# Decoder of two layers on one core: the first attention's value products one step later behind their moves, a layer norm one group later, and the rest of an entmax eight products into the experts' first step

## The chip, the cores and the metric

The kernel runs on one core of one Trainium2 chip. A core has five engines with a queue of instructions each: TensorE (PE, matrix products; its loads of stationary operands are listed as PEld), VectorE (DVE), ScalarE (ACT), GpSimd (POOL) and SyncE (SP, which here only issues transfers). Transfers (DMAs) are issued from SP or ACT and moved by 16 DMA engines. The metric is the device time of one execution in microseconds (us), lower is better; the figure of a kernel is the median of its runs. One further execution is recorded by the hardware profiler, and that is the profile and trace read here.

## The reference, cut to what matters

Two sequences of 1024 tokens of width 256 pass through six blocks, each followed by a residual and a layer norm, all in float32: attention, cross attention with an MLP, a mixture of experts, then attention, cross attention and a quantised MLP. The change touches the first three.

```
x = layernorm(x + attn(x))        # attn(x) itself returns x + z
    q, k, v = 16 heads of 64;  weights = softmax(q k^T / 8);  z = (weights v) w_o
x = layernorm(x + xattn(x, ctx))  # one head, 64 context tokens
    out = softmax(q k^T) v;  gelu(out W1 + b1) W2 + b2
x = layernorm(x + experts(x))     # 8 experts, hidden width 1024
    gates = entmax(x Wr + br)     # alpha = 1.5, by bisection
    y_e = relu(x W1_e + b1_e) W2_e + b2_e;  out = sum_e gates_e y_e
```

## The kernel before, in words

**First attention (`l0_attn`, L206).** The 16 heads of a sequence are taken two at a time; such a pair of heads of one sequence is a unit `u`, 16 in all. A unit has eight steps of 128 queries; there are 128 steps `n`. A step's work for its 128 queries and both heads is:

- `scores`: eight matrix products into two wide PSUM tiles (L297);
- `most`: two row maxima on DVE (L312); `exponentials`: two exponentials on ACT, with row sums (L317); `divided`: a reciprocal on DVE (L325) and two divisions on POOL (L328);
- `turn`: two transposes of 32 by 32 blocks on DVE into `blocks` (L342), of which there are two buffers, each for two steps.

Two steps make one pair `m`. After the second step's `turn`, `move` brings the 32 by 32 blocks into place for a product, `turned`, of which there are two buffers too: of sixteen copies over partitions twelve are DMAs of 128 KB (ten issued from SP, L358, two from ACT, L360), two are copies on POOL (L362), and two are kept for `stays`, which does one on ACT (L367) and one on POOL (L368) a step later. `mix(m)` is the value product: 32 products of PE into one PSUM bank `acc` (L379), evacuated by ACT into `aoT` (helper L74).

`others` holds work that is due at a numbered step (the `at(...)` calls): the projections of q and k of the next unit, one 512-token block at a time (`project`, L252), each followed by two DMAs from SP that shift one head's rows to the other half of the partitions (L266, for k only after its second block); its values (L276); weight loads from SP (L237); output products (L396) whose sums DVE takes (L402, L404); the layer norm's `finish`, and `onward`, the transposes of a normed group for the next stage (helpers: moments L178 to L183, the power L183 on POOL, scaling L200, transposes on PE L157).

The main loop (L490 to L509) writes this order out by hand for PE, DVE, ACT and POOL. At step `n` it emits `scores`, `most` and `exponentials` of `n + 2`, `turn` of `n + 1`, `divided` of `n + 2`; and then by parity:

```
if n % 2:
    stays()
    mix((n - 3) // 2)
else:
    others(n - 1)
    others(n)
    move(n + 1)
```

So pair `m` is moved at step 2m and multiplied at step 2m + 3. Below, a step is called even or odd by this `n`. SP's queue takes its DMAs in the order of this text. The last `mix` and four outputs are kept in `self.left_over`, and the last two groups' `finish` and `onward` in `self.ends`.

**Cross attention (`l0_xattn`, L577).** Four groups `g` of 512 tokens. PE's order is by hand: first layer `up` (L648) in four pieces, second layer `down` (L661, sums on DVE L665) in four pieces, with the next group's softmax, transposes and value products between them. The entmax of the first sequence's router (`entmax`, L740 on) is a generator that yields between stretches of DVE work; `self.rest` is that generator. In group 2 the kernel takes four stretches of it by `some()`; the third ends with a power on POOL (L791), and the next on DVE begins with L793, which reads it.

**Experts (`l0_ffn`).** 32 steps (8 experts by 4 groups), each with 21 places in a hand-written order of products; at a place, a job from a table can be put behind the product. At step 0 the table holds the rest of the first entmax, the last group's transposes and router product (`last_group`), and four pieces of `begin(0)`, which turns the gates on PE (L873) and starts the accumulators. `tokens` prepares the groups' Strassen sums.

Of the kernel before, what the change touches and what calls it, by code (L numbers as in the profile page):

```python
# [33 lines left out]
class Decoder:  # L34
# [181 lines left out]
    def l0_attn(self):  # L216
# [5 lines left out]
        with ExitStack() as s:  # L222
# [123 lines left out]
            def move(n):  # L346
                m, qt = divmod(n, 2)
                if qt == 0 or not 0 <= n < steps:
                    return
                to = turned[m] = tp.tile([P, 8, 4, P], F32, tag="turned", name="turned")  # L350
                src = blocks.pop(m).rearrange("p (k r) h t q -> p k r (h t q)", r=4)
                moves = [
                    (to[32 * r : 32 * r + 32, :, i, :], src[32 * i : 32 * i + 32, :, r, :])
                    for d in range(4) for i in range(4) for r in [(i + d) % 4]
                ]
                few = 6 if n == steps - 1 else 2
                for b, a in moves[4 : 16 - few]:
                    nc.sync.dma_start(b, a)  # L358
                for b, a in moves[16 - few :]:
                    nc.scalar.dma_start(b, a)  # L360
                for b, a in moves[:2]:
                    nc.gpsimd.tensor_copy(b, a)  # L362
                stay.extend(moves[2:4])
# [6 lines left out]
            def mix(m):  # L370

                if m < 0:
                    return
                u, qb = divmod(m, 4)
                av = self.acc()
                for kt in range(8):
                    p = turned[m][:, kt].rearrange("p i (h t q) -> p h i t q", h=2, t=2)
                    for h in range(2):
                        nc.tensor.matmul(  # L379
                            av[own[h], 0:256].rearrange("p (t i q) -> p i t q", t=2, i=4),  # L380
                            lhsT=vals[u][:, kt, own[h]], rhs=p[:, h], start=kt == 0, stop=kt == 7,
                        )
                if qb == 0:
                    aT[u] = aop.tile([P, S], F32, tag="aoT", name="aoT")
                self.evac(aT[u][:, qb * 256 : (qb + 1) * 256], av[:, 0:256], by=nc.scalar)
# [36 lines left out]
            steps = B * NP * 8  # L422
# [38 lines left out]
            def others(n):  # L461
                for f, args in extra.pop(n, ()):
                    f(*args)
# [5 lines left out]
            with self.tc.manual_schedule(engines=engines):  # L469
                def begin(n):  # L470
                    scores(n)
                    for f in (most, exponentials):
                        for h in range(2):
                            f(n, h)
                    divided(n)

                for n in (-12, -11):
                    others(n)
                for k, i in ((1, 0), (1, 1), (0, 0)):
                    project(0, k, i)  # L480
                begin(0)
                project(0, 0, 1)
                for n in (-10, -8, -6, -4, -2):
                    others(n)
                for i in range(2):
                    values(0, i)
                begin(1)
                for i in range(2, 4):
                    values(0, i)
                for h in range(2):  # L490
                    turn(0, h)
                nc.sync.dma_start(wo, t["L0_attn_w_o"].rearrange("(g p) d -> p g d", p=P))
                next(constants)
                for n in range(steps):
                    scores(n + 2)
                    for h in range(2):
                        most(n + 2, h)
                        exponentials(n + 2, h)
                    for h in range(2):
                        turn(n + 1, h)  # L500
                    divided(n + 2)
                    if n % 2:
                        stays()
                        mix((n - 3) // 2)
                    else:
                        others(n - 1)
                        others(n)
                        move(n + 1)
            assert not extra  # L509

            self.left_over = [lambda: mix(steps // 2 - 1)] + [
# [65 lines left out]
    def l0_xattn(self):  # L577
# [5 lines left out]
        with ExitStack() as s:  # L583
# [113 lines left out]
            with self.tc.manual_schedule(engines={mybir.EngineType.PE}):  # L697
                with self.tc.high_priority(400):
                    softmax(0)
                    for job in self.left_over:  # L700
                        job()
                    turn(0)
                    mix(0)
                queries(0)
                for g in range(NG):
                    up(g, 0)
                    up(g, 2)
                    some()
                    onward(g - 1)
                    queries(g + 1)  # L710
                    some()
                    if g == 0:
                        for job in self.ends:
                            job()
                    up(g, 4)
                    softmax(g + 1)
                    some()
                    up(g, 6)
                    logits(g - 1)
                    if g > 0:  # L720
                        self.xT[g - 1] = xT[g - 1]
                    if g in (1, 2):
                        self.tokens(g - 1)
                    if g == 2:
                        self.rest = self.entmax(0)
                        steps = islice(self.rest, 4)
                    some()
                    down(g, 0)
                    turn(g + 1)
                    some()  # L730
                    down(g, 1)
                    mix(g + 1)
                    some()
                    down(g, 2)
                    some()
                    down(g, 3)
# [101 lines left out]
    def l0_ffn(self):  # L838
        nc, t = self.nc, self.t
        HT = GT // 2  # L840
        with ExitStack() as s:
# [157 lines left out]
            with self.tc.manual_schedule(engines=engines):  # L999
                start = [begin(b) for b in range(B)]  # L1000
                mixed = None
                for n in range(len(steps) + 1):
                    jobs = {}
                    for k in range(4):
                        if n == 3:
                            jobs[k] = lambda: next(start[1])
                    if n == 0:
                        jobs[0] = lambda: [None for _ in self.rest]
                        jobs[3], jobs[6] = self.last_group
                        for k in range(7, 11):  # L1010
                            jobs[k] = lambda: next(start[0])
                    for k in {1: (4, 7, 10, 13), 2: (8, 12)}.get(n, ()):
                        jobs[k] = lambda: next(gates)
                    if n > 3:
                        jobs[14] = lambda: next(ready, None)
                    if n >= len(steps) - NG + 2:
                        g = n - (len(steps) - NG + 2)
                        if n < len(steps):
                            jobs[5], jobs[17] = (lambda: normed(g)), (lambda: turned(g))
                    a = hidden(*steps[n]) if n < len(steps) else None  # L1020
                    b = gather(*steps[n - 1], mixed) if n else None
                    if n % NG == 1 and n // NG + 1 < E:
                        load(n // NG + 1)
                    for i, k in enumerate(order):
                        if isinstance(k, int):
                            if b:
                                b(k)
                        elif a:
                            a(*k)
                        if i in jobs:  # L1030
                            jobs[i]()
                    if n == 0:
                        for _ in start[0]:
                            pass
                        self.tokens(2)
                        self.tokens(3)
                    if n == 2:
                        for _ in gates:
                            pass
                    if n % NG == NG - 1 and n // NG + 1 < E:  # L1040
                        first(n // NG + 1)
                    if n % NG == 0 and 0 < n < len(steps):
                        second(n // NG)
                    if a:
                        mixed = sums(*steps[n])
                for _ in ready:
                    pass
                for g in range(2, NG):
                    normed(g)
# [743 lines left out]
```

## Time and profile before

| | us |
|---|---|
| median of 3 runs | 2489.21 (2487.06 to 2491.77) |
| profiled execution | 2493.86 |
| its span in the trace | 2492.0 |
| mean granted clock of PE | 0.968 |
| PE busy, of the span | 2346.6 |
| DVE, ACT, POOL busy | 1686.2, 1107.1, 909.8 |

The span runs from the first to the last instruction in the trace; the 1.9 us beside it are start and end of the execution. The stages and PE's busy time in them:

| stretch of the span (us) | what runs there | PE busy (us) | share of the DMA engines |
|---|---|---|---|
| 0 to 40 | loads, first projections | 30.08 | 0.63 |
| 40 to 787 | first attention | 705.27 of 747 | 0.81 |
| 787 to 957 | first cross attention | 158.13 of 170 | 0.09 |
| 957 to 1560 | experts | 600.58 of 603 | 0.07 |
| 1560 to 2492 | second layer | 852.56 of 932 | 0.13 |

How the page and the trace's answers are read: in a group's row stand line, engine, operation, written tile, read tile, shapes and count, then busy time and the mean of one in ns, then the engine's idle time ahead of these instructions and what ended most of it. A row of waits has engine, tile and line, then what it waited for, then us in total, times and the longest; "SPq" is SP's queue. A row of the timeline begins with start and duration in us and ends with the idle time before it and what ended it, in brackets. A row of transfers ends with the size and the median us from issue to landing.

### The profile page before, as it was taken

To read this page: it belongs to the slowest core of one execution; us is meant where nothing else is said; L and a number is where in the kernel's file an instruction comes from. 1 tells how busy PE (TensorE), PEld (TensorE's weight loads), DVE (VectorE), ACT (ScalarE), POOL (GpSimd) and SP (SyncE) were. 2 spreads that over 40 slices of the span, in tenths; PEclk is the share of its full clock that TensorE was granted. 3 is DMA by queue.
4 is the path that set the end of the run, shared out by engine and by line. 5 is a ranking of instruction groups with operands and counts; after the bars stand their busy time and mean duration, and the time that the engine had idled before them with its cause. 6 is when DMAs were issued, how large, how long until landed. Compare 5 with 4: busy or idle time off the path is not lost. (4 is left out here: it accounts for less than half of the span.)

```text
span 2492.0 us, 37380 instructions
## 1 busy us (share of the span) xinstructions
PE 2346.6 (94%) x14062; PEld 1603.8 (64%) x14065; DVE 1686.2 (68%) x2934; ACT 1107.1 (44%) x1730; POOL 909.8 (37%) x747
## 2 busy tenths in 40 slices
PE   8999999999998989999999999999889999998974
PEld 4455545455555658899999999999734444444742
DVE  5888788887784334555555555546678787985786
ACT  4565565565552212233333333333136555663344
POOL 4666666566566122342343342423201001002412
PEclk9999999999999999999999999999979999999995
DMA  7888788787887001010010010100212222300001
GB/s 166 163 160 165 152 174 169 139 164 153 161 161 165 1 0 41 1 39 26 13 35 30 18 46 1 47 5 1 42 26 35 35 35 35 53 16 1 1 1 34
DMA packets 275668, 168.79 MB, mean 68 GB/s; under 512 B 47560, under 2 KB 262176, under 8 KB 275488
## 3 DMA queue, kind: packets, MB, share of 16 engines
q1 hardware_dynamic: 239072, 148.05, 28.6%
q10 hardware_dynamic: 36416, 18.36, 3.7%
q8 instruction: 111, 1.82, 0.3%
q14 instruction: 69, 0.57, 0.1%
HBM read 34.21 MB, written 2.10 MB: 15 GB/s over the span
## 5 line engine op out<-in xcount | busy, mean ns | idle before, releaser
L312 DVE TENSOR_REDUCE nm<-wide 128x1 f32<-128x1024 f32 x256 | 301.3, 1218 | 121.9 <-PE wide L297 120.2
L1160 DVE TENSOR_REDUCE most<-bank 128x1 f32<-128x512 f32 x512 | 325.6, 683 | 56.4 <-PE bank L1154 48.0
L1203 ACT ACTIVATE w<-wide 128x1024 f32<-128x1024 f32 x256 | 248.3, 1022 | 139.1 <-PE wide L1197 130.5
L379 PE MATMUL acc<-turned,v 128*64 128x256 f32 x2048 | 241.3, 389 | 30.0 <-DMA turned<-blocks 14.7
L297 PE MATMUL wide<-k,q 64*128 64x512 f32 x1024 | 258.4, 619 | 9.0 <-ACT p L317 8.3
L317 ACT ACTIVATE p<-wide,nm 128x1024 f32<-128x1024 f32 x128 | 142.6, 1114 | 238.1 <-DVE nm L312 150.0
L328 POOL TENSOR_SCALAR p<-p,sums 128x1024 f32<-128x1024 f32 x128 | 143.2, 1118 | 276.7 <-DVE sums L325 276.7
L379 PEld LDWEIGHTS acc<-turned,v 128*64 128x64 f32 x2048 | 155.5, 140 | 136.4 <-issue 42.7
L906 ACT ACTIVATE mhT<-mhT,cols 128x256 f32<-128x256 f32 (+1 forms) x256 | 143.1, 607 | 141.5 <-DVE mhT L934 98.2
L817 POOL TENSOR_TENSOR hs<-hs,mhT 128x1024 f32<-128x1024 f32 x31 | 102.2, 3297 | 242.6 <-DVE hs L815 242.6
L917 PE MATMUL unit<-xT,w 128*128 128x256 f32 x768 | 182.4, 380 | 0.0
L974 DVE SCALAR_TENSOR_TENSOR r<-acc,gates,r 128x128 f32<-128x128 f32 x256 | 77.7, 345 | 140.7 <-PE acc L965 140.7
L297 PEld LDWEIGHTS wide<-k,q 64*128 64x128 f32 x1024 | 88.5, 187 | 125.3 <-issue 94.6
L342 DVE STREAM_TRANSPOSE blocks<-p 128x1024 f32<-128x1024 f32 x128 | 157.9, 1234 | 11.1 <-DMA turned<-blocks 4.5
L1154 PE MATMUL bank<-kst,qst 64*128 64x512 f32 x512 | 148.9, 483 | 12.7 <-DVE most L1160 12.1
L183 POOL TENSOR_TENSOR rstd<-ve,nhalf 128x4 f32<-128x4 f32 (+2 forms) x28 | 26.1, 931 | 363.0 <-DVE ve L181 362.6
L342 DVE STREAM_TRANSPOSE blocks<-r 128x1024 f32<-128x1024 f32 x128 | 153.8, 1201 | 0.0
L917 PEld LDWEIGHTS unit<-xT,w 128*128 128x128 f32 x768 | 141.0, 190 | 17.2 <-issue 0.7
L1154 PEld LDWEIGHTS bank<-kst,qst 64*128 64x128 f32 x512 | 70.0, 193 | 122.4 <-DVE most L1160 96.2
L328 POOL TENSOR_SCALAR r<-r,sums 128x1024 f32<-128x1024 f32 x128 | 143.3, 1120 | 0.0
L317 ACT ACTIVATE r<-wide,nm 128x1024 f32<-128x1024 f32 x128 | 141.8, 1108 | 0.3 <-issue 0.2
L1217 PE MATMUL acc<-w,v 128*32 128x512 f32 x1024 | 137.8, 610 | 0.0
(327 smaller groups left out, 4543.2 us busy)
## 6 DMA issues: line engine op xcount, KB each, us to landing
turned<-blocks SPq DMA_DIRECT2D x636, 128.0 KB, 2.8
turned<-blocks ACTq DMA_DIRECT2D x132, 128.0 KB, 3.5
w<-in_L_ffn_W SPq DMA_DIRECT2D x16, 1024.0 KB, 5.4
q<-q SPq DMA_DIRECT2D x64, 128.0 KB, 2.4
k<-k SPq DMA_DIRECT2D x32, 128.0 KB, 3.1
qst<-qh SPq DMA_DIRECT2D x60, 64.0 KB, 2.4
qst<-ql SPq DMA_DIRECT2D x60, 64.0 KB, 2.4
kst<-kh SPq DMA_DIRECT2D x60, 64.0 KB, 2.8
```

The source lines that it names most:

```text
L297: nc.tensor.matmul(sc[h][:, kb, :], lhsT=q[rows, qi, at : at + P], rhs=k[rows, ki, :], start=True, stop=True,)
L312: nc.vector.tensor_reduce(nm, sc, AX.XY, ALU.max, negate=True)
L317: nc.scalar.activation(p, sc.rearrange("p a c -> p (a c)"), AF.Exp, bias=nm, accum_out=sums[:, 0, h : h + 1],)
L328: nc.gpsimd.tensor_scalar(p, p, sums[:, 1, h : h + 1], 1.0, ALU.mult, ALU.mult)
L342: nc.vector.transpose(blocks[m][:, :, h, qt, :], p.rearrange("p (j q) -> p j q", q=32))
L379: nc.tensor.matmul(av[own[h], 0:256].rearrange("p (t i q) -> p i t q", t=2, i=4), lhsT=vals[u][:, kt, own[h]], rhs=p[:, h], start=kt == 0, ...
L906: nc.scalar.activation(hT[:, f, cols], hT[:, f, cols], AF.Relu, bias=self.cols[:, col : col + 1])
L917: nc.tensor.matmul(v[:, m, :], lhsT=up[e][k][:, f : f + P], rhs=self.halves[g][k], start=k in (1, 2, 5) and m == 0, stop=True, skip_group_ ...
L1154: nc.tensor.matmul(sc[a], lhsT=stack[b, jp, "q"][rows, q0 : q0 + P], rhs=stack[b, jp, "k"][rows, kb * 512 : (kb + 1) * 512], start=True, s ...
L1160: nc.vector.tensor_reduce(most[n][:, kb, qt, h : h + 1], sc[a], AX.X, ALU.max, negate=True)
L1203: nc.scalar.activation(slot[:, k, :], ps[k].rearrange("p a q -> p (a q)"), AF.Exp, scale=0.25)
L1217: nc.tensor.matmul(mixed[n][o : o + 32, :], lhsT=vals[b][:, kt, 17 * h : 17 * h + 32], rhs=pT[:, a, :], start=kt == 0, stop=kt == 7, tile_ ...
```

## The change

Three places are edited.

First, in the loop of the first attention: `others` goes from the even to the odd steps, and `mix` from the odd to the even, behind `move`. Pair `m` is now multiplied at step 2m + 4 instead of 2m + 3, and one `mix` more follows the loop. Work due at an even step is emitted one step later, and work due at an odd step one earlier.

Second, in the cross attention: of the two entries of `self.ends`, one is done in group 0 and one in group 1, instead of both in group 0.

Third, in step 0 of the experts: the rest of the entmax goes from place 0 to place 7, the two jobs of `last_group` from places 3 and 6 to 5 and 8, and the four pieces of `begin(0)` from 7 to 10 to 11 to 14.

```diff
                     divided(n + 2)
                     if n % 2:
                         stays()
-                        mix((n - 3) // 2)
-                    else:
                         others(n - 1)
                         others(n)
+                    else:
                         move(n + 1)
+                        mix(n // 2 - 2)
+                mix(steps // 2 - 2)
             assert not extra
...
                     some()
-                    if g == 0:
-                        for job in self.ends:
-                            job()
+                    if g < 2:
+                        self.ends[g]()
                     up(g, 4)
...
                     if n == 0:
-                        jobs[0] = lambda: [None for _ in self.rest]
-                        jobs[3], jobs[6] = self.last_group
-                        for k in range(7, 11):
+                        jobs[5], jobs[8] = self.last_group
+                        jobs[7] = lambda: [None for _ in self.rest]
+                        for k in range(11, 15):
                             jobs[k] = lambda: next(start[0])
```

In the order that results on the engines, DVE's L793 and the entmax work behind it stand in the experts' first step, after the last layer norm of the cross attention; before, they stood between the first and the second sum (L665) of group 2.

## Prediction

> **What bounds the kernel now.** I read the page's busy shares first, then its groups, the waits of the engines and of SP's queue in the first stage, and last the timeline around each long gap.
>
> The page of the kernel before:
>
> ```profile
> PE 2346.6 (94%) x14062; PEld 1603.8 (64%) x14065; DVE 1686.2 (68%) x2934; ACT 1107.1 (44%) x1730; POOL 909.8 (37%) x747
> ...
> L379 PE MATMUL acc<-turned,v 128*64 128x256 f32 x2048 | 241.3, 389 | 30.0 <-DMA turned<-blocks 14.7
> ...
> turned<-blocks SPq DMA_DIRECT2D x636, 128.0 KB, 2.8
> turned<-blocks ACTq DMA_DIRECT2D x132, 128.0 KB, 3.5
> ```
>
> TensorE (PE) is busy 94% of the span, so a change of order can only win PE's gaps. The value products (L379) have the largest: 30.0 us before 64 groups. Waits of PE, then of SP's queue, from 30 to 800 us (us in total, times, longest):
>
> ```profile
> PE acc L379 <- DMA turned<-blocks: 14.7, 9, 3.4
> PE wide L297 <- ACT p L317: 7.7, 5, 2.7
> PE acc L379 <- DMA q<-q: 6.3, 3, 4.6
> ...
> PE acc L379 <- POOL turned L368: 3.5, 1, 3.5
> ```
>
> ```profile
> SPq L358 <- DMA turned<-blocks: 52.1, 41, 3.2
> SPq L266 <- ACT k L74: 49.1, 15, 6.9
> SPq L266 <- ACT q L76: 21.8, 9, 4.3
> ```
>
> SP issues the shifts of k and q (L266) ahead of the ten moves of a step, and a shift waits for a projection of that same step: 49.1 + 21.8 us in which the moves stand behind it. That is why they land late. PE's timeline shows what lateness costs, clock included:
>
> ```profile
> 573.88 5.36 PE L379 MATMUL acc<-turned,v 128*64 128x256 f32 x32 [4.60 <-DMA q<-q]
> ...
> 585.81 3.67 PE L379 MATMUL acc<-turned,v 128*64 128x256 f32 x32
> ...
> 779.96 6.54 PE L379 MATMUL acc<-turned,v 128*64 128x256 f32 x32 [3.48 <-POOL turned L368]
> ```
>
> DVE is nearly as full; its one idle time in a clean pair of steps is this:
>
> ```profile
> 352.07 2.36 DVE L312 TENSOR_REDUCE nm<-wide 128x1 f32<-128x1024 f32 x2 [0.84 <-PE wide L297]
> ```
>
> Two later places matter. PE at the end of the first attention, then all engines at the second layer product of the cross attention:
>
> ```profile
> 810.77 0.33 PE L157 MATMUL bank<-ident,xg 128*128 128x128 f32 x1 [1.81 <-DVE xg L200]
> 811.69 1.41 PE L157 MATMUL bank<-ident,xg 128*128 128x128 f32 x7 [0.59 <-DVE xg L200]
> 812.94 5.29 PE L648 MATMUL wide<-xoT,w 128*128 128x512 f32 x8
> ```
>
> ```profile
> 903.47 10.55 POOL L791 TENSOR_TENSOR esq<-u,eroot 128x64 f32<-128x64 f32 x1 [0.88 <-DVE u L790]
> ...
> 914.05 0.23 DVE L793 TENSOR_TENSOR esq<-emean,esq 128x64 f32<-128x64 f32 x1 [10.33 <-POOL esq L791]
> ...
> 917.30 9.65 PE L661 MATMUL bank<-w,xhT 128*128 128x256 f32 x32 [8.64 <-DVE r L665]
> ```
>
> The entmax's power on POOL takes 10.55 us; DVE's L793 waits for it, and L665, which frees PE's bank, is queued behind L793. PE stands 8.64 us and then runs 32 products in 9.65 us instead of the 7.17 of the other rows.
>
> **What the Trainium skill says.** "Perfetto Trace Analysis", Tensor Engine Instruction: ACT, DVE and GpSimd queues are strictly first in, first out. The trace agrees: L665 was ready after its product ended near 906.7 and ran at 916.83. "TensorE: Matmul & The Clock Gate", What's actually happening: an idle window of about 3.4 us halves PE's clock. The trace agrees in kind: after gaps of 4.60, 3.48 and 8.64 us the products took 1.69, 2.87 and 2.48 us more. "DMA: Bandwidth & Descriptors", Anatomy of one DMA: about 2 us fixed plus bytes over 436 GB/s, so an estimate of 2.3 us for 128 KB; the trace has 2.8 and 3.5, and I use those.
>
> **Part A, the loop of the first attention.** Nothing is added or removed; per pair of steps PE still does two scores (2 × 1.92), 32 value products (3.60), a projection (1.8) and values (1.0): 10.25 us, as the mixes at 347.29, 357.54 and 367.78 show; some 48 of 64 pairs are such, the rest have outputs too and no gaps. Let T be the end of the step's transposes. Before, the products wanted the moves at T+11.1, and they landed at T+10 to 13. After, mix m comes one step later, and I count T+16.7. The shifts go to the other step, so SP starts the moves without a projection ahead of them. What it meets instead: in the order of the changed program the first moves or the shift often need the semaphore lane of ACT's two moves of the same step, which land about T+3.2 and T+4.75 (issue T+0.1 and T+0.7 plus 3.5, and queueing). So SP starts at T+3.9 to 5.4; its ten issues and the landing took 8.5 to 10 us before; landing T+13 to 14.3. Slack at the products: 2.4 us or more.
> - Gaps gone: 30.0 − 3.48 (the last) = 26.5; the slow clock at 573.88, 1.7.
> - The end: POOL took L183 and constants ahead of the last copies; now the copies come directly after the transposes. 3.48 + 2.87 = 6.35 goes. A gap of 1.77 before the last scores is filled by a mix. Gross −36.3.
> - Given back, fill: one more step before the first mix, +0.7 (0.5 to 1).
> - Given back, the second shift of q: 11 of 15 units wait for the ACT moves' lane, landing T+5.7 to 6.4 where PE wants it at T+5.95; 0 to 0.5 us each, with lag more: +4 (0 to 8).
> - Given back, `blocks`: two buffers, so the transposes of two pairs on want the moves landed at T+13.46. Landing at 13 to 14.3 stalls DVE 0 to 0.85 us; its slack is the 0.84 us of a pair shown above. +4 (0 to 10).
> - New wait: with two `turned` buffers the moves of m+2, written ahead of mix m, wait for that mix. It ends at 5.59 us after the step's start and the transposes end at 5.75, so it costs nothing on time; if PE lags, ACT's two moves hold the evacuation (L74) and exponentials behind them, and SP and POOL start late by as much. With other leftovers (five waits of scores for ACT, 7.7 us, may grow or shrink): +4 (−3 to 8).
> Sum A: −36.3 + 0.7 + 4 + 4 + 4 = −23.6 (−36 to −9).
>
> **Part B, the second `ends`.** Finish and onward of group 3 move one group later, beside PE's eight transposes there. Gone: 1.81 + 0.59 + (5.29 − 3.60) = 4.1. The same DVE scaling stands at the later place, where DVE has room (29.7 busy of 90 us from 790 to 880): −3.5 (−4.1 to 0).
>
> **Part C, the entmax.** After, L793 stands in the experts' first step, behind the last norm. Gone: 8.64 + 2.48 = 11.1. Eleven DVE operations of 0.22 us, 2.6 us, move into that step; DVE is busy 55.7 of 103 us there while PE is at 101.7, and the gate transposes on PE come four places later in turn: I count gates ready 9 us into the step and wanted at 10.9. POOL's L183 behind the power has about 3 us of room. −10.5 (−11.1 to −8). Without that cover the price is PE waiting for the gates, up to 3 us.
>
> Sum: −23.6 − 3.5 − 10.5 = −37.6 on the profiled execution, 2493.86 us (span 2492.0), 4.65 above the median. I take the difference off the median: **2452**.
>
> **Rivals.**
> - *A is paid in full.* Nothing given back but the fill: −35.6 − 4.1 − 11.1 = −51, 2438. For: the measured slack on DVE. Against: the lanes.
> - *A wins nothing.* The transfer was only moved: gaps pass from L379 to L297 (shifts, ACT) and L342. B and C alone, −14: 2475. For: DVE already waits 4.5 us for moves at L342, and its slack is thin. Against: nine gaps of PE had the moves themselves as cause.
> - *Slower, by one loop.* SP's moves held behind ACT's landings, pair after pair, so that transposes wait for `blocks`. From T+15.2 on (13.46 plus two pairs' slack of 1.7) each us of landing adds 0.5 us to a pair, 24 us over 48 pairs. At T+16.7 the whole gain is gone; at T+17.2 it is +11: 2500. The upper ends give 5.4 + 8 + 3.2 = T+16.6, so it needs every move late; not excluded, since ACT's moves land later whenever ACT lags.
> - *The change doesn't do what it says.* The order within each engine is that of the program text here, so all three moves happen; what can fail is their worth.
>
> **How the numbers follow.** Likeliest case (2444 to 2464) 0.45; in full 0.2; nothing from A 0.2; the loop 0.12; near no change 0.03. Within 0.2%, 5 us, is about what a measurement of this kernel can tell from no change. Faster 0.85, same 0.03, slower 0.12. The range from 2434 to 2484 holds the first three cases with the bounds of A (−36 to −9), B and C, and leaves out the loop and a little at each side. Both signs do not share the chance evenly; the likeliest case's own range is 2444 to 2464.
>
> **What would show it.** Right: L379's idle time falls from 30.0 to a few us; SP's waits for ACT k and q (70.9 us) nearly vanish and those for DMA grow; the last mix takes 3.67 us without a gap; at the second-layer product no gap of 8.64 us, and L793 stands in the experts' stage. Wrong: L342's idle time on DVE, 11.1 us in its first row, grows to 50 or more with DMA as its releaser; L297 gains idle time on q or on ACT; PE's pairs are over 10.6 us in the stretches without outputs; gate transposes make PE wait in the experts' first step.

## The result: 7.4 us faster, a fifth of what was forecast

The median went from 2488.91 us (six runs, 2487.06 to 2491.77) to 2481.51 us (six runs, 2473.99 to 2483.07): 0.9966 of the time before, 95% interval 0.9953 to 0.998. The profiled execution took 2483.07 us with a span of 2481.3, against 2493.86 and 2492.0. The forecast was 2452, with a range of 2434 to 2484.

The page of the changed kernel, busy shares and three groups (columns as before):

```profile
PE 2359.1 (95%) x14062; PEld 1594.6 (64%) x14065; DVE 1683.4 (68%) x2934; ACT 1109.7 (45%) x1730; POOL 910.9 (37%) x747
...
L297 PE MATMUL wide<-k,q 64*128 64x512 f32 x1024 | 272.4, 628 | 16.9 <-ACT p L317 13.6
...
L379 PE MATMUL acc<-turned,v 128*64 128x256 f32 x2048 | 236.4, 384 | 2.4 <-ACT aoT L74 1.6
...
L342 DVE STREAM_TRANSPOSE blocks<-p 128x1024 f32<-128x1024 f32 x128 | 158.0, 1235 | 47.1 <-DMA turned<-blocks 17.0
```

Two of these groups before the change:

```profile
L297 PE MATMUL wide<-k,q 64*128 64x512 f32 x1024 | 258.4, 619 | 9.0 <-ACT p L317 8.3
...
L342 DVE STREAM_TRANSPOSE blocks<-p 128x1024 f32<-128x1024 f32 x128 | 157.9, 1234 | 11.1 <-DMA turned<-blocks 4.5
```

The value products lost their gaps, 30.0 to 2.4 us. But the scores (L297) wait 16.9 us instead of 9.0 and run 14.0 us longer (272.4 against 258.4), and DVE stands idle for 47.1 us ahead of the transposes (L342) instead of 11.1. SP's queue in the first attention (30 to 800 us) shows what the moves, which read the transposes' buffers, are waiting for:

```profile
SPq L266 <- DMA turned<-blocks: 73.2, 26, 5.9
SPq L237 <- DMA turned<-blocks: 68.3, 24, 6.6
SPq L358 <- DMA turned<-blocks: 34.3, 23, 5.5
```

The waits for projections (70.9 us) are gone as foreseen. In their place SP waits 175.8 us for moves to land, in 73 waits. Before, the moves' own such waits were the 52.1 us shown in the prediction, the shifts (L266) had none, and the weight loads had these:

```profile
SPq L237 <- DMA turned<-blocks: 16.8, 10, 3.7
```

That is 68.9 us together. A shift of q or a weight load reads nothing of a move. But the DMAs of the program as built raise eight completion semaphores in turn, and each is issued only when the transfer eight DMAs back, which raised the same one, has landed. By these semaphores, 72 of the 73 waits (175.6 us) are for one of the two moves that ACT issues. One such case on its way to PE, from the timeline of all engines (DVE's transposes of that pair had ended at 344.38):

```profile
344.53 1.29 ACTq L360 DMA_DIRECT2D turned<-blocks  x2
...
348.12 0.89 SPq L237 DMA_DIRECT2D wv<-in_L_attn_w_v  x2
...
349.33 3.98 SPq L358 DMA_DIRECT2D turned<-blocks  x6
...
360.26 1.25 DVE L342 STREAM_TRANSPOSE blocks<-p 128x1024 f32<-128x1024 f32 x1 [3.02 <-DMA turned<-blocks]
...
362.60 2.33 DVE L312 TENSOR_REDUCE nm<-wide 128x1 f32<-128x1024 f32 x2
...
363.90 1.11 ACT L317 ACTIVATE p<-wide,nm 128x1024 f32<-128x1024 f32 x1 [2.79 <-DVE nm L312]
...
365.16 2.26 PE L297 MATMUL wide<-k,q 64*128 64x512 f32 x8 [1.13 <-ACT p L317]
```

ACT's two moves land at 348.11 and 349.25; the weight load has the semaphore of the first, SP's first move that of the second. So SP's moves begin 4.95 us after the transposes, and the last of them lands at 360.18. The transpose of two pairs on, which needs the buffer, stands 3.02 us; the maxima behind it are late, so are the exponentials, and PE's scores stand 1.13 us. (The granted clock is 1.00 there.)

The other places of the prediction, in PE's timeline of the changed kernel and, for L793, in DVE's:

```profile
787.83 3.67 PE L379 MATMUL acc<-turned,v 128*64 128x256 f32 x32 [0.52 <-issue]
...
802.23 8.69 PE L649 MATMUL wide<-xoT,w 128*128 128x512 f32 x16
...
815.37 3.60 PE L649 MATMUL wide<-xoT,w 128*128 128x512 f32 x8
...
824.03 3.62 PE L662 MATMUL bank<-w,xhT 128*128 128x256 f32 x16
...
910.55 7.17 PE L662 MATMUL bank<-w,xhT 128*128 128x256 f32 x32
```

```profile
953.49 0.22 DVE L793 TENSOR_TENSOR esq<-emean,esq 128x64 f32<-128x64 f32 x1
```

Before, the first layer's first and the second layer's first products stood here:

```profile
796.79 7.13 PE L648 MATMUL wide<-xoT,w 128*128 128x512 f32 x16
...
823.29 3.62 PE L661 MATMUL bank<-w,xhT 128*128 128x256 f32 x16
```

The last value products no longer stand 3.48 us and run slow; the first layer's products behind the transposes take 3.60 instead of 5.29 us; the second layer's have no gap; and L793 waits for nothing, in the experts' first step.

For an account, the span of the profiled execution is cut at four starts in PE's timeline: the first value product of the first pair (mix 0), that of pair 60, the left-over outputs behind the last pair, and the experts' first product (L917; L916, L918 or L920 where the edit shifts lines). The median is that of all runs of a kernel; the kernels below the first two are those of the experiments. All in us:

| kernel | median | mix 0 at | mix 0 to mix 60 | mix 60 to outputs | outputs to experts | experts to end |
|---|---|---|---|---|---|---|
| before | 2488.91 | 46.81 | 699.82 | 39.80 | 170.56 | 1535.04 |
| after | 2481.51 | 51.10 | 699.83 | 40.50 | 156.34 | 1533.51 |
| second and third part only | 2475.17 | 46.85 | 700.55 | 39.10 | 154.75 | 1534.31 |
| first part only | 2498.16 | 49.98 | 705.89 | 35.54 | 172.19 | 1534.94 |
| after, mix ahead of move | 2473.12 | 50.92 | 699.55 | 33.83 | 155.12 | 1537.77 |
| after, stays late | 2471.58 | 51.06 | 693.24 | 37.49 | 154.74 | 1533.85 |
| after, both | 2464.31 | 50.39 | 689.78 | 34.13 | 154.74 | 1536.74 |
| after, all moves on SP | 2446.53 | 50.97 | 673.31 | 33.00 | 154.76 | 1534.09 |
| after, four moves on ACT | 2529.53 | 54.07 | 751.81 | 34.59 | 154.75 | 1533.95 |
| after, a copy of ACT for its moves | 2446.65 | 50.83 | 672.65 | 33.48 | 154.77 | 1537.38 |
| parts two and three, all on SP | 2468.62 | 45.87 | 694.49 | 37.80 | 154.77 | 1532.88 |
| after, all on SP, both | 2439.08 | 50.03 | 664.53 | 33.43 | 154.75 | 1534.56 |

So the gain of the profiled execution, 10.7 us, is 14.2 us between the outputs and the experts' start and 1.5 behind it, less 5.0 us that the first attention lost.

### The profile page after: what moved, and what is told of

The parts are those of the page before. It is cut to its first block, busy times and chain, and to the rows that moved or that the text cites. A ratio compares the mean times of both kernels' runs of the same rounds, so it can differ in the third digit from the quotient of the medians.

```text
span 2481.3 us, 37321 instructions
## 1 busy us (share of the span) xinstructions
PE 2359.1 (95%) x14062; PEld 1594.6 (64%) x14065; DVE 1683.4 (68%) x2934; ACT 1109.7 (45%) x1730; POOL 910.9 (37%) x747
## 5 line engine op out<-in xcount | busy, mean ns | idle before, releaser
L297 PE MATMUL wide<-k,q 64*128 64x512 f32 x1024 | 272.4, 628 | 16.9 <-ACT p L317 13.6
L379 PEld LDWEIGHTS acc<-turned,v 128*64 128x64 f32 x2048 | 143.2, 137 | 114.8 <-issue 34.0
L342 DVE STREAM_TRANSPOSE blocks<-p 128x1024 f32<-128x1024 f32 x128 | 158.0, 1235 | 47.1 <-DMA turned<-blocks 17.0
L297 PEld LDWEIGHTS wide<-k,q 64*128 64x128 f32 x1024 | 90.5, 188 | 144.1 <-issue 74.8
L917 PE MATMUL unit<-xT,w 128*128 128x256 f32 x768 | 182.3, 380 | 0.0
L342 DVE STREAM_TRANSPOSE blocks<-r 128x1024 f32<-128x1024 f32 x128 | 153.8, 1202 | 0.0
L917 PEld LDWEIGHTS unit<-xT,w 128*128 128x128 f32 x768 | 140.9, 190 | 16.9 <-issue 0.3
```

Of the source, the lines that this page charges most:

```text
L297: nc.tensor.matmul(sc[h][:, kb, :], lhsT=q[rows, qi, at : at + P], rhs=k[rows, ki, :], start=True, stop=True,)
L342: nc.vector.transpose(blocks[m][:, :, h, qt, :], p.rearrange("p (j q) -> p j q", q=32))
L379: nc.tensor.matmul(av[own[h], 0:256].rearrange("p (t i q) -> p i t q", t=2, i=4), lhsT=vals[u][:, kt, own[h]], rhs=p[:, h], start=kt == 0, ...
L917: nc.tensor.matmul(v[:, m, :], lhsT=up[e][k][:, f : f + P], rhs=self.halves[g][k], start=k in (1, 2, 5) and m == 0, stop=True, skip_group_ ...
```

## The experiments

**The parts alone.** One kernel has the second and third part with the old loop, one the new loop with the rest as before. Each is the change's diff without the other's lines.

> The second and third part alone, the loop of the first attention as before. Theory (the parts add; the traces put -14.2 us between the left-over outputs and the experts' first product, and +5.0 us in the first attention): 2488.9 - 14.2 = 2474.7 us, 7 us faster than with all three parts; from the left-over outputs to the first product of the experts 156 us. Rival (the first part earns something that the cross attention's start hides): no faster than with all three parts, 2481 us or more.

Measured: 2475.17 us, 0.9936 (0.9924 to 0.9948) of before, as expected; 154.75 us from outputs to experts. The same two places of the cross attention:

```profile
796.86 7.13 PE L648 MATMUL wide<-xoT,w 128*128 128x512 f32 x16
...
817.51 3.62 PE L661 MATMUL bank<-w,xhT 128*128 128x256 f32 x16
```

> The first part alone. Theory: its gaps are gone from L379 (30 us to under 4 us) but stand elsewhere, so the end of the first attention comes 3 to 6 us later than before: 2492 to 2495 us. Rival (the prediction's sum): -24 us, 2465 us.

Measured: 2498.16 us, 1.0027 (1.0017 to 1.0037) of before, 7.9 us slower than before in the same round, somewhat more than expected; its value products have 2.6 us of idle time, its transposes 43.7 between 40 and 800 us. The parts add up: −15.1 and +7.9 give −7.2, measured −7.4. The first part by itself makes this kernel slower.

**The last step.** ACT's queue at the end of the changed kernel, then PE:

```profile
766.75 6.86 ACTq L360 DMA_DIRECT2D turned<-blocks  x6
773.65 0.37 ACT L74 COPY aoT<-acc 128x256 f32<-128x256 f32 x1 [12.31 <-DMA turned<-blocks]
...
775.12 1.27 ACT L574 ACTIVATE xg<-bank,cols 128x512 f32<-128x512 f32 x2
```

```profile
774.08 0.70 PE L396 MATMUL bank<-wo,aoT 128*128 128x256 f32 x2 [2.29 <-ACT aoT L74]
```

The value products of pair 61 were done at 761.8, but their evacuation is written behind the six moves that ACT issues for the last pair; the outputs need it, and two more banks wait for the query evacuations (L574). PE's granted clock is 0.50 from 774.7 to 784.9 us.

```diff
                     else:
-                        move(n + 1)
                         mix(n // 2 - 2)
+                        move(n + 1)
```

> All three parts, with mix written ahead of move in the even step. Theory (at the end ACT issues the six moves of the last pair ahead of the evacuation of aoT and of the query products, and PE's outputs wait for both): the evacuation no longer waits 12.3 us behind the moves, PE's gaps between the last scores and the last two mixes shrink from 5.5 us to under 1 us, with slow clock 6 to 8 us off: 2474 to 2476 us; the pairs before the end as they were. Rival (the end is bound by DVE's sums L404 and the moves' landing): within 2 us of 2481.5 us.

Measured: 2473.12 us, 0.9927 (0.9914 to 0.994) of before. The stretch from mix 60 to the outputs falls from 40.50 to 33.83 us, that from mix 0 to mix 60 stays (699.83, 699.55). The evacuation now comes 5.8 us ahead of the moves:

```profile
760.68 0.37 ACT L74 COPY aoT<-acc 128x256 f32<-128x256 f32 x1
766.49 5.78 ACTq L360 DMA_DIRECT2D turned<-blocks  x6
```

The gaps of the outputs did not fall under 1 us as expected: three waits for DVE's sums, 2.2 us together, remain. The sum of the stretch went as expected; the granted clock is 1.00 from 740 to 785 us.

**The odd step.** `others` now shares the step with `stays`, and ACT's copy stands ahead of the evacuations that free PE's banks. The changed kernel's timeline:

```profile
148.38 1.04 ACT L367 COPY turned<-blocks 32x1024 f32<-32x1024 f32 x1
...
149.45 0.60 ACT L76 ACTIVATE q<-bank 128x512 f32<-128x512 f32 x1
...
150.10 1.11 PE L157 MATMUL bank<-ident,xg 128*128 128x128 f32 x4 [2.36 <-ACT q L76]
```

```diff
                     if n % 2:
-                        stays()
                         others(n - 1)
                         others(n)
+                        stays()
```

> All three parts, with stays written behind others in the odd step, so that ACT's copy of 1.04 us (L367) stands behind the evacuations of projections and values. Theory (PE's waits for banks in the odd step, twice 2.36 us before transposes of x and about 1 us before outputs, come from that copy): each shrinks by about 1 us, with the slow clock 3 to 6 us off: 2475 to 2479 us. Rival (only the wait for the two block buffers counts): L342's idle time stays at 47 us and the time within 2 us of 2481.5 us.

Measured: 2471.58 us, 0.9922 (0.9909 to 0.9935) of before, better than expected. The wait above in this kernel:

```profile
147.66 0.66 PE L157 MATMUL bank<-ident,xg 128*128 128x128 f32 x4 [1.16 <-ACT q L76]
```

It shrank by 1.2 us, and the four products behind it take 0.66 instead of 1.11: the granted clock, 0.50 from 150.1 to 153.4 us in the changed kernel, is 1.00 in this one. Mix 0 to mix 60 shrank by 6.6 us, while L342's idle time stayed at 48.4 us between 40 and 800 us. So this cause stands beside that of the transposes. With both edits together:

> All three parts, with mix written ahead of move in the even step and stays behind others in the odd step. Theory (two separate causes, ACT's queue at the end and ACT's copy in the odd steps; part of either gain was at the end, so they overlap): 2467 to 2471 us, faster than either alone. Rival (both edits do the same, they only let ACT evacuate earlier): no faster than the better of them, 2471.6 us.

Measured: 2464.31 us, 0.9904 (0.9887 to 0.992) of before, a little under the expected band. They are two causes: against the changed kernel's 2481.51 the edits save 8.4 and 9.9 us alone and 17.2 together.

**Who issues the moves.** The main suspicion was SP's 175.8 us of waits for landings. In the first kernel ACT issues none of the moves except the last pair's six; in the second it issues four a pair.

```diff
-                few = 6 if n == steps - 1 else 2
+                few = 6 if n == steps - 1 else 0
```

> All three parts, with the two moves that ACT issues given to SP, the last pair as it was. Theory (SP's moves start about 4.2 us after the transposes because they, or the shift or load ahead of them, wait for the landing of ACT's two): they now start within 1 us of the transposes, and although SP issues twelve, they land 2 us earlier; the idle time of the transposes L342 falls from 47 to under 25 us and the time by 4 to 10 us: 2472 to 2478 us. Rival (landing is set by the rate at which SP issues, 0.66 us each): landing not earlier, L342's idle time stays and the time is 2481 us or more.

Measured: 2446.53 us, 0.9829 (0.9814 to 0.9843) of before, far more than the 4 to 10 us expected. The page's row of the value products, and of SP's waits the only row that still names a landing:

```profile
L379 PE MATMUL acc<-turned,v 128*64 128x256 f32 x2048 | 235.7, 383 | 0.8 <-POOL rstd L183 0.5
```

```profile
SPq L358 <- DMA turned<-blocks: 5.4, 2, 4.1
```

175.8 us became 5.4. SP's first move is issued 0.5 us after the transposes end (median of pairs 1 to 59) instead of 4.1, and the last one lands 11.1 us after that end instead of 13.6, though SP issues twelve. (A landing is taken from the last raise of the move's semaphore in the trace.) L342's idle time is 4.7 us between 40 and 800 us. Almost every pair without outputs now takes 10.25 us.

> All three parts, with four of the moves issued by ACT instead of two (the last pair has six as before). Theory (SP waits for ACT's landings): SP's first move starts about 1.3 us later, SP has two fewer to issue, so the landing stays where it was and the time is within 3 us of 2481.5 us or slower, since ACT spends 1.3 us more in the even step ahead of the evacuation. Rival (SP's issue rate sets the landing): landing 1.3 us earlier, L342's idle time under 30 us, 2474 to 2478 us.

Measured: 2529.53 us, 1.0158 (1.0143 to 1.0173) of before; both expectations failed. SP starts 0.06 us after the transposes (median), the last move lands 10.5 us after their end, and no transpose waits for it, yet nearly every such pair takes 11.3 to 11.4 us. Here it is ACT's own queue:

```profile
332.74 3.77 ACTq L360 DMA_DIRECT2D turned<-blocks  x4
...
336.55 0.37 ACT L74 COPY aoT<-acc 128x256 f32<-128x256 f32 x1 [4.46 <-PE bank L276]
...
336.82 1.12 ACT L317 ACTIVATE p<-wide,nm 128x1024 f32<-128x1024 f32 x1
...
338.08 2.22 PE L297 MATMUL wide<-k,q 64*128 64x512 f32 x8 [0.75 <-ACT p L317]
```

Four issues take 3.77 us beside SP's, the exponentials behind them start late, and PE's scores wait for them 47 times, 46.8 us, between 40 and 800 us. This left a doubt about two moves as well: does the run with none gain by SP's waits, or by the 1.3 us that ACT no longer spends? A kernel for that: SP has eleven, and ACT makes the twelfth itself as a copy, at the same place and with the same waits.

```diff
+                few = 6 if n == steps - 1 else 1
...
                 for b, a in moves[16 - few :]:
-                    nc.scalar.dma_start(b, a)
+                    if few == 1:
+                        nc.scalar.copy(b, a)
+                    else:
+                        nc.scalar.dma_start(b, a)
```

> All three parts; of the two moves that ACT issued, one goes to SP (eleven there) and one is made by ACT itself as a copy, at the same place in its queue and with the same waits (an ACT copy of this size, L367, takes 1.04 us; the two issues took 1.3). No DMA of ACT is left before the last pair. Theory (what cost the time was SP waiting for the landing of ACT's moves): SP starts within 1 us of the transposes, L342's idle time stays under 15 us, and the time is within 8 us of the run with all on SP: 2446 to 2454 us. Rival (it was the time that ACT spends there ahead of the evacuation and the exponentials): 2470 us or more.

Measured: 2446.65 us, 0.9834 (0.9821 to 0.9848) of before, the same as with all on SP. The copy stands where the issues stood, nearly as long (1.04 us against some 1.3), and costs nothing:

```profile
342.55 1.04 ACT L361 COPY turned<-blocks 32x1024 f32<-32x1024 f32 x1 [1.13 <-PE acc L382]
343.60 0.37 ACT L74 COPY aoT<-acc 128x256 f32<-128x256 f32 x1
344.60 1.11 ACT L317 ACTIVATE p<-wide,nm 128x1024 f32<-128x1024 f32 x1 [0.63 <-DVE nm L312]
```

The exponentials still wait for DVE behind it, not for ACT. So with two moves it is SP's waits for their landing that cost the time, not what ACT spends on issuing them.

**Is the later product worth anything?** The old loop, with the second and third part, and all moves on SP:

> The second and third part, the loop of the first attention as before, with all moves but the last pair's on SP. Theory (the later value product is worth its gaps once SP no longer waits for ACT's moves, and only then): the shifts still stand ahead of the moves in SP's queue and twelve moves land later than ten, so the value products keep 25 to 45 us of idle time: 2470 to 2490 us, 24 us or more above the same with the first part. Rival (giving the moves to SP is a gain of its own, with or without the first part): 2450 us or less.

Measured: 2468.62 us, 0.9919 (0.9905 to 0.9932) of before, just under the expected band, and 22.1 us above the same with the first part, where 24 or more was expected. Its value products still have gaps, and its shifts still wait for the step's projection:

```profile
L379 PE MATMUL acc<-turned,v 128*64 128x256 f32 x2048 | 236.6, 383 | 28.2 <-DMA q<-q 9.1 <-DMA wq<-in_L_attn_w_q 5.2 <-DMA turned<-blocks 4.4
```

```profile
SPq L266 <- ACT k L74: 53.4, 15, 8.4
```

The first part costs 6.3 us where ACT issues two moves (2475.17 to 2481.51) and saves 22.1 where it issues none.

**The three edits together.** All moves on SP, `mix` ahead of `move`, `stays` behind `others`:

> All three parts, all moves but the last pair's on SP, mix ahead of move, stays behind others. Theory (what is left of the first attention's gaps with all on SP, some 12 us, is the last step and the banks that ACT frees late in the odd steps): 2436 to 2442 us. Rival (with the landing early those waits no longer reach PE): within 3 us of 2446.5 us.

Measured: 2439.08 us, 0.9803 (0.9789 to 0.9816) of before: faster than both kernels, 42.4 us below the changed one.

## Why the prediction was wrong, step by step

- *Parts B and C* were right. The sum was −14.0 us; the traces give −14.2, and the two alone −15.1 by the medians. For B, the stretch from the first layer's first product (L648, now L649) to the first second-layer product was 26.50 us and is 21.80, less 1.2 to 1.4 for the transposes that group 1 now has: −3.3 to −3.5. That this meets the −3.5 is in part luck. With the second and third part alone the stretch is 20.65 us, a gain of some 4.5, over the upper bound of 4.1; in the changed kernel the first sixteen products took 8.69 instead of 7.13 us, at a granted clock of 0.50 from 802.0 to 805.4 us. For C the gap of 8.64 us and the slow products are gone (9.65 to 7.17), and the gates cost PE 0.25 us at their transposes' sums.
- *Part A's gross gain* was right as a mechanism. The value products' gaps went from 30.0 to 2.4 us, and with SP free of the landings the stretch from mix 0 to mix 60 is 26.5 us shorter. That this is the sum 30.0 − 3.48 of the prediction to the tenth is chance: giving the moves to SP takes 6.1 us off the same stretch without the first part (700.55 to 694.49), and the first part takes 21.2 off it on top (694.49 to 673.31).
- *The step that failed is what part A gives back in its body*: +4 for the shifts, +4 for `blocks`, +4 for the rest, 12 us. It gave back all of the 28.2 us forecast there (26.5 and the 1.7 of the slow clock): mix 0 to mix 60 takes 699.83 us, and took 699.82. The wait was named and its place was right; its size was not. Landing was put at T+13 to 14.3, though the prediction's own terms (start at T+3.9 to 5.4, then 8.5 to 10) reach from T+12.4 to 15.4, and DVE's slack at 0.84 us a pair. In the trace the last move of a pair lands at T+13.6 (median of pairs 1 to 59), so the middle was right; but a quarter land after T+14.7 and the latest at T+16.1. Where 0 to 0.85 us was put on each pair, the transposes stalled 23 times by 0.15 to 3.41 us, 43.5 us in all; each time they began 0.08 to 0.32 us after the last move of two pairs earlier had landed. Before, there were five such stalls, 7.5 us in all. (The remaining 3.6 us of either kernel are a wait for POOL in the last pair.) I had set a typical landing against a typical slack, where each late pair counts for itself.
- *A term was missing*: `stays` ahead of `others` in the odd step. Moving it out of the way is worth 9.9 us by the medians (2481.51 to 2471.58), 6.6 of them between mix 0 and mix 60.
- *The end* was put at −8.1 us (6.35 and 1.77). Mix 60 to the outputs became 0.7 us longer. It did so although one step's scores fewer stand in it (1.92 us). The prediction named ACT's moves ahead of the evacuation as a cost when PE lags, but priced two of them, not the six of the last pair; mix ahead of move takes 6.7 us off that stretch.
- *The fill* was put at +0.7. Mix 0 starts 4.29 us later; the scores of one step, 1.92 us, are then done that were left at the end before, so the net is 2.4 us.
- *The rivals.* "A wins nothing" (2475) came closest, with its mechanism: the gaps passed to L297 and L342. The loop that was to make it slower was there, in some pairs only; all moves on SP take 26.5 us off the body, against the 48 that the loop was to cost at T+17.2.
- *A slip in the sum.* The lower ends of part A's terms add up to −38.8 us, not −36. It doesn't bear on the outcome.

What stays open is how the waiting SP reaches PE in shares. L342's idle time went from 47.1 to 4.7 us with the waits, and the stalls follow the landings pair by pair, so the two `blocks` buffers are the likely main way; but late shifts of q (1.9 us of PE's waits) went at the same moment. A third buffer of `blocks`, which would tell, wasn't tried.

## What to carry to other kernels

When a consumer is given a step more of time, look at what the freed producer's buffers gate next, and compare the latest landing with the slack of one round, not the mean with the mean. A queue can wait for a transfer that it has no data from, through a shared completion semaphore; a few transfers issued from a second queue can therefore hold the first one back, as ACT's two moves a pair did here. And when work changes parity, list what each engine's queue already has in that step: here a copy of 1.04 us ahead of the evacuations cost ten.

## What was unexpected of the hardware

Two queues issued hardly faster than one here. With all twelve moves on SP the issues of a pair took 7.96 us (median), 0.66 each; with eight on SP and four on ACT the eight alone took 7.89, with 0.8 us between ACT's and 1.0 between SP's (medians), though SP waited for a landing ahead of its moves only 0.2 us in all. Where ACT issues two a pair, they stand 0.63 us apart. So giving four moves to ACT shortened nothing, and cost ACT 3.77 us in the pair shown.
